# Attention scores on TensorE: two 64x128 matmuls per tile, or eight of 64x32

## The chip, the cores and the metric

The kernel runs on one core of a Trainium2 chip. The metric is the device time of one execution in microseconds (us); it is given as the median of several runs. A profile is of one execution. The engines are called as the profile calls them: PE (TensorE, matmuls), PEld (its weight loads), DVE (VectorE), ACT (ScalarE), POOL (GpSimd) and SP (SyncE, which only issues DMAs here). All data are fp32.

## What is computed

One layer with two residual blocks on x of shape (2, 2048, 256): a layer norm with a tanh recurrence, then a layer norm with an attention whose values and outputs are mixed from five small experts by top-2 gates. The change is in the attention, whose reference is, cut to what matters:

```python
q = (x @ Wq).reshape(b, t, h, dh).transpose(0, 2, 1, 3)      # 8 heads of 64
k = (x @ Wk).reshape(b, t, h, dh).transpose(0, 2, 1, 3)
...
v = jnp.einsum('bthe,btek->bhtk', wv, xv)
scores = jnp.einsum('bhid,bhjd->bhij', q * scale, k)
probs = jax.nn.softmax(scores, axis=-1)
attn = jnp.einsum('bhij,bhjd->bihd', probs, v)
...
out = jnp.einsum('bthe,bthk,ekd->btd', mask_o, attn, Wo)
```

## The kernel before

The recurrence comes first and takes about the first 130 us. The rest is the attention: 2 batches x 8 heads = 16 heads, each with 4 query blocks (QB = 512 queries), so 64 units. A unit runs over the 2048 keys in HC = 8 score tiles of 256 keys; there are 512 tiles.

A score tile `s` is [128, 2, 512] in PSUM: keys on partitions, two key blocks of 128 side by side (`o` = 0, 1), 512 queries. A head has only 64 features, so the 128 rows of the array are used as two halves. `keys` (L140) writes the keys of even blocks to partitions 0 to 63 of `k` and those of odd blocks to partitions 64 to 127. `queries` (L159) keeps `q` with one query block in the lower and another in the upper half, and `qs`, the same with the halves exchanged by two DMAs on SP's queue. So in `scores` (L634) the block `o` = 0 uses the lower 64 rows of the array and `o` = 1 the upper 64, with `q` or `qs` as the moving operand; each half has all 128 columns of the array for its 128 keys. The two halves write to different halves of the tile's second axis.

What then happens to a tile:

- `stage` (L645, ACT) copies it to SBUF as `p`, and `largest` (L655, DVE) keeps a running maximum over the unit's tiles, straight from PSUM.
- At a unit's end the maximum is turned (`pm`, L668, PE), reduced (L673, DVE) and spread again (`pt`, L683, PE; `top`, L686, ACT).
- Some turns later `subtract` (L693, POOL, some on DVE) and `exponential` (L696, ACT) make the probabilities in place.
- `products` (L706, PE) multiplies them by the values: per tile eight matmuls of 128 rows x 32 columns, four column quarters at a time, summed into `o` over the unit.
- `fold` (L718, a DMA on POOL's queue that adds in SBUF) adds two tiles of probabilities, and `sums` (L727, PE, 128 x 32 as well) takes the denominators `d` of the folded ones.
- A unit's result is turned (`po`, L759), weighed by the gates (L772) and added up in DRAM.

The order on all engines is written out by hand. The loop makes one turn for every two tiles: it issues the scores of two new tiles, then copies, maxima, subtractions, the listed extra work (`before`), `products` of two tiles from LAG = 6 turns earlier, `sums`, and more extra work (`behind`): `keys` (`pk`), `queries` (`pq`), `experts` (`pv`), transposes. Each engine takes its instructions in that order. There are 256 such turns. On PE a pair of score tiles stands therefore between matmuls of 128 x 32 (`o`, `d`, `pk`, `pq`, `pv`) or transposes of 128 x 128 (`pm`, `pt`, `po`). `s` has two buffers in PSUM (4 of the 8 banks); a new tile waits until ACT and DVE are done with the one two before it.

Of the kernel before, what the change touches and what calls it, by code (L numbers as in the profile page):

```python
# [14 lines left out]
P = 128  # L15
# [5 lines left out]
def rnn_then_switchhead_kernel(  # L21
# [15 lines left out]
    nc = tc.nc  # L37
    B, T, D = x.shape
    E, _, DH = Wv.shape
# [85 lines left out]
    k_of, q_of = {}, {}  # L125
# [502 lines left out]
    def scores(t):  # L628
        i, n = units[t // HC]
        c = t % HC  # L630
        ss = ps_s.tile([P, 2, QB], F32, tag="s", name=f"s{t}")
        for o in range(2):
            half = slice(o * DH, (o + 1) * DH)
            nc.tensor.matmul(  # L634
                ss[:, o, :],
                lhsT=k_of[i][half, c, :],
                rhs=q_of[i, n][o][half, :],
                start=True,
                stop=True,
            )  # L640
        return ss

    def stage(t, ss):
# [359 lines left out]
    with tc.manual_schedule():  # L1003
        for T in range(NT + LAG + 1):
# [8 lines left out]
            if old:  # L1013
                exponential(old[1])

            ss = [scores(t) for t in new]
            if new:
                stage(new[0], ss[0])
# [88 lines left out]
```

## Time and profile before

| | us |
|---|---|
| median of 5 runs (lowest, highest) | 1617.29 (1614.42, 1619.65) |
| the profiled execution | 1613.42 |
| its span, first to last instruction | 1611.7 |
| PE busy, matmuls | 1535.6 |
| L634, scores, busy (each half of the rows) | 512 |
| L706, products, busy | 491.5 |
| L727, sums, busy | 153.0 |
| L693, subtractions on POOL, busy | 1054.7 |

The profiled execution is 3.9 us below the median. Busy times of one engine's groups can overlap: two halves of the rows, or quarters of the columns, that run at once are each counted in their own group. A matmul's row in the trace gives its start well; its end is modelled. A shape such as 64*128 64x512 means 64 rows and 128 columns of the array, with 512 columns of 64 partitions moving. A releaser behind an arrow is what ended an engine's idle time.

### The profile page before, as it was taken

Reading aid. Unit: us, or ns where it says so; the run is one execution under the profiler, and the core shown is the slowest. Engines: PE = TensorE matmul, PEld = TensorE weight load, DVE = VectorE, ACT = ScalarE, POOL = GpSimd, SP = SyncE. Lnnn points to the kernel's source line nnn. Section 1 sums busy time; section 2 is a strip of 40 time slices with the busy share of each in tenths; the row PEclk is TensorE's granted clock in tenths of the full one; section 3 lists DMA queues with packets and bytes.
Section 4 is the critical chain, followed back from the end, with each engine's and each line's share of the span. In section 5 each row is a group of like instructions: output and inputs, shape, how many; then the busy total and the mean of one; then the engine's idle time right before and its main releaser. Section 6 shows DMA issues by size and latency. Waiting matters only on the chain.

```text
span 1611.7 us, 29233 instructions
## 1 busy us (share of the span) xinstructions
PE 1535.6 (95%) x11442; PEld 590.0 (37%) x11442; DVE 1297.6 (81%) x1808; ACT 1251.1 (78%) x1617; POOL 1283.4 (80%) x856
## 2 busy tenths in 40 slices
PE   6989899999999999999999999999999999999996
PEld 5974233333233333333334333333333333333233
DVE  7473889998988888888977769898989888888762
ACT  4664688888788888888887778888888888888861
POOL 3044698898888888999997868898989898889970
PEclk9999999999999999999999999999999999999999
DMA  5021468788888878778886767788888888888852
GB/s 162 1 106 32 117 156 196 162 187 163 183 170 167 179 161 176 162 172 164 176 184 157 168 142 187 156 177 174 177 166 174 177 169 172 165 170 165 171 131 86
DMA packets 86623, 252.26 MB, mean 157 GB/s; under 512 B 11920, under 2 KB 31184, under 8 KB 86480
## 3 DMA queue, kind: packets, MB, share of 16 engines
q0 software_dynamic: 43200, 163.60, 54.0%
q1 hardware_dynamic: 41648, 86.13, 17.2%
q8 instruction: 91, 1.49, 0.4%
q10 hardware_dynamic: 1632, 0.61, 0.1%
q14 instruction: 52, 0.43, 0.1%
HBM read 59.46 MB, written 50.33 MB: 68 GB/s over the span
## 4 chain that ended last, share of the span: by engine, by line
PE 66%; DVE 12%; DMA 7%; ACT 3%; issue 2%; POOL 2%; SPq 0%; DVEq 0%; ACTq 0%; POOLq 0%
PE s L634 23%; PE o L706 20%; PE d L727 6%; DMA p<-p 5%; DVE m L655 5%; PE pk L140 4%; PE pq L159 3%; ACT p L645 2%; PE pz L846 2%; DVE pro L772 2%; PE pt L683 2%; POOL p L693 1%; PE pm L668 1%; PE po L759 1%; PE pv L574 1%
## 5 line engine op out<-in xcount | busy, mean ns | idle before, releaser
L693 POOL TENSOR_TENSOR p<-p,top 128x1024 f32<-128x1024 f32 x381 | 1054.7, 3010 | 11.8 <-ACT top L686 11.7
L645 ACT COPY p<-s 128x1024 f32<-128x1024 f32 x512 | 510.9, 1011 | 152.5 <-DVE m L655 64.6
L696 ACT ACTIVATE p<-p 128x1024 f32<-128x1024 f32 x512 | 538.2, 1062 | 49.4 <-DVE p L693 37.3
L634 PE MATMUL s<-qs,k 64*128 64x512 f32 x1024 | 511.8, 617 | 6.4 <-ACT p L645 6.3
L634 PE MATMUL s<-q,k 64*128 64x512 f32 x1024 | 511.9, 617 | 3.9 <-ACT p L645 3.2
L706 PE MATMUL o<-p,v 128*32 128x512 f32 x4096 | 491.5, 597 | 10.2 <-DVE os L743 7.8
L655 DVE TENSOR_TENSOR m<-s,m 128x1024 f32<-128x1024 f32 x320 | 390.9, 1221 | 95.5 <-PE s L634 86.9
L718 POOL DMA_DIRECT2D p<-p x252 | 338.1, 1342 | 61.7 <-PE o L706 21.6
L706 PEld LDWEIGHTS o<-p,v 128*32 128x32 f32 x4096 | 113.6, 109 | 297.8 <-issue 155.3
L634 PEld LDWEIGHTS s<-qs,k 64*128 64x128 f32 x1024 | 169.0, 185 | 144.4 <-ACT p L645 46.2
L634 PEld LDWEIGHTS s<-q,k 64*128 64x128 f32 x1024 | 169.1, 185 | 138.6 <-issue 52.1
L693 DVE TENSOR_TENSOR p<-p,pt 128x1024 f32<-128x1024 f32 x131 | 158.5, 1210 | 0.1
L727 PE MATMUL d<-p,ones 128*32 128x512 f32 x1040 | 153.0, 593 | 5.0 <-DMA p<-p 4.9
L655 DVE TENSOR_TENSOR m<-s,p 128x1024 f32<-128x1024 f32 x64 | 78.4, 1224 | 55.3 <-ACT p L645 54.9
L814 POOL DMA_DIRECT2D yd<-pro x48 | 45.0, 937 | 91.7 <-DVE pro L772 89.4
L772 DVE TENSOR_TENSOR pro<-po,mr 128x1280 f32<-128x1280 f32 (+1 forms) x67 | 95.9, 1431 | 2.7
L619 DVE TENSOR_TENSOR xq<-xq,wp 128x1280 f32<-128x1280 f32 x60 | 89.3, 1488 | 2.3 <-DVE wp L617 0.2
L625 DVE TENSOR_REDUCE v<-xq 128x256 f32<-128x1280 f32 x60 | 88.6, 1477 | 0.0
L727 PEld LDWEIGHTS d<-p,ones 128*32 128x32 f32 x1040 | 37.2, 110 | 97.3 <-issue 77.5
L159 PE MATMUL pq<-xn2T,wq 128*32 128x512 f32 x512 | 63.2, 612 | 6.7 <-DVE rootd L434 6.7
L140 PE MATMUL pk<-xn2T,wk 128*32 128x512 f32 x512 | 61.5, 598 | 0.0
L673 DVE TENSOR_REDUCE mq<-pm 128x4 f32<-128x512 f32 x64 | 44.3, 692 | 18.3 <-PE pm L668 16.9
(172 smaller groups left out, 1468.5 us busy)
## 6 DMA issues: line engine op xcount, KB each, us to landing
p<-p POOLq DMA_DIRECT2D x252, 512.0 KB, 6.0
xq<-xvd SPq DMA_DIRECT2D x60, 640.0 KB, 5.4
yd<-pro POOLq DMA_DIRECT2D x48, 640.0 KB, 7.1
qs<-q SPq DMA_DIRECT2D x64, 128.0 KB, 2.7
yd<-pro SPq DMA_DIRECT2D x8, 640.0 KB, 4.1
y<-yd SPq DMA_DIRECT2D x8, 640.0 KB, 6.7
x<-in_x SPq DMA_DIRECT2D x16, 256.0 KB, 5.6
x1d<-x SPq DMA_DIRECT2D x16, 256.0 KB, 2.0
```

The source lines that it names most:

```text
L140: nc.tensor.matmul(pk[at_col : at_col + 32], lhsT=wk[:, kc, h * DH + g : h * DH + g + 32], rhs=xc[:, kc, c0 // 2 : (c0 + HC) // 2, o, :], ...
L159: nc.tensor.matmul(pq[at_col : at_col + 32, :], lhsT=wq[:, kc, h * DH + g : h * DH + g + 32], rhs=xn2T[:, kc, b, n * QB : (n + 1) * QB], s ...
L619: nc.vector.tensor_tensor(xq, xq, wp.unsqueeze(2).to_broadcast([P, 4, DH, E]), ALU.mult)
L634: nc.tensor.matmul(ss[:, o, :], lhsT=k_of[i][half, c, :], rhs=q_of[i, n][o][half, :], start=True, stop=True,)
L645: nc.scalar.copy(p, ss)
L655: nc.vector.tensor_tensor(m, ss, ring[t - 1] if c == 1 else m, ALU.max)
L693: eng.tensor_tensor(p, p, top.unsqueeze(1).to_broadcast([P, 2, QB]), ALU.subtract)
L696: nc.scalar.activation(ring[t], ring[t], AF.Exp)
L706: nc.tensor.matmul(o_of[u][at_col : at_col + 32, :], lhsT=v_of[i][:, 2 * c + o, g : g + 32], rhs=ring[t][:, o, :], start=c == 0, stop=c == ...
L718: nc.gpsimd.dma_start(out=ring[t], in_=ring.pop(t + 1), accum_op=ALU.add)
L727: nc.tensor.matmul(den_of[u][32 * g : 32 * (g + 1), :], lhsT=ones32, rhs=ring[(t, t1)[g // 2]][:, g % 2, :], start=first, stop=last, tile_ ...
L772: nc.vector.tensor_tensor(dst, po[:, s : s + n, 0:DH].unsqueeze(2).to_broadcast([P, n, E, DH]), mr[:, s : s + n].unsqueeze(3).to_broadcast ...
```

## The change

The matmul of each half is cut into four of 32 keys. Each writes 32 partitions of the score tile and is given its place in the array: row 0 or 64, and column 0, 32, 64 or 96. The same numbers are computed.

```diff
         for o in range(2):
             half = slice(o * DH, (o + 1) * DH)
-            nc.tensor.matmul(
-                ss[:, o, :],
-                lhsT=k_of[i][half, c, :],
-                rhs=q_of[i, n][o][half, :],
-                start=True,
-                stop=True,
-            )
+            for g in range(0, P, 32):
+                nc.tensor.matmul(
+                    ss[g : g + 32, o, :],
+                    lhsT=k_of[i][half, c, g : g + 32],
+                    rhs=q_of[i, n][o][half, :],
+                    start=True,
+                    stop=True,
+                    tile_position=(o * DH, g),
+                )
         return ss
```

## The prediction

> **What bounds the kernel now.** I read the page first, for who is busy and what the chain of waits is made of.
>
> ```profile
> span 1611.7 us, 29233 instructions
> ...
> PE 1535.6 (95%) x11442; PEld 590.0 (37%) x11442; DVE 1297.6 (81%) x1808; ACT 1251.1 (78%) x1617; POOL 1283.4 (80%) x856
> ...
> PE 66%; DVE 12%; DMA 7%; ACT 3%; issue 2%; POOL 2%; SPq 0%; DVEq 0%; ACTq 0%; POOLq 0%
> PE s L634 23%; PE o L706 20%; PE d L727 6%; DMA p<-p 5%; DVE m L655 5%; PE pk L140 4%; PE pq L159 3%; ACT p L645 2%; PE pz L846 2%; DVE pro L772 2%; PE pt L683 2%; POOL p L693 1%; PE pm L668 1%; PE po L759 1%; PE pv L574 1%
> ```
>
> The reader is to see that PE holds two thirds of the chain and that the changed line, L634, is its largest piece. Since a busy PE is not PE at its peak, I then asked for the busy times of the attention stretch alone (its columns: length, then busy time and count of PE, PEld, DVE, ACT and POOL, granted clock, DMA share, GB/s).
>
> ```profile
> 133.00:1545.00 1412.00, 1373.81 (x10059) 470.70 (x10063) 1191.68 (x1422) 1152.12 (x1374) 1219.22 (x782) 1.00 0.78 165
> ```
>
> PE stands still for 1412.0 - 1373.8 = 38.2 us of it (2.7%); the next engine, POOL, is free for 193 us. The granted clock is 1.00 throughout, so nothing is throttled. A nanosecond taken from PE's own sequence here is worth about 0.97 ns. Next the timeline of PE, for what its sequence costs beyond the streaming of columns; each row is start, length, engine, line, names, rows*columns of the array.
>
> ```profile
> 815.35 0.69 PE L634 MATMUL s<-q,k 64*128 64x512 f32 x1
> 815.35 0.69 PE L634 MATMUL s<-qs,k 64*128 64x512 f32 x1
> 815.88 0.59 PE L634 MATMUL s<-q,k 64*128 64x512 f32 x1
> 815.89 0.59 PE L634 MATMUL s<-qs,k 64*128 64x512 f32 x1
> 816.31 0.59 PE L634 MATMUL s<-q,k 64*128 64x512 f32 x1
> ...
> 816.74 0.59 PE L634 MATMUL s<-q,k 64*128 64x512 f32 x1
> ...
> 817.26 1.92 PE L140 MATMUL pk<-xn2T,wk 128*32 128x512 f32 x16
> ```
>
> Every matmul of the code is two passes in the trace (2048 records of s for 1024 instructions), each with its own weight load. The two row halves, q and qs, run side by side 7 ns apart, so a score tile costs two rounds, and a pair of tiles four. By the records' starts to the nanosecond, rounds follow each other after 429 ns (815.88 to 816.31), except the first (534) and the step out to pk (526). In the weight loads the same stretch reads:
>
> ```profile
> 815.35 0.18 PEld L634 LDWEIGHTS s<-q,k 64*128 64x128 f32 x1 [0.84 <-ACT p L696]
> ...
> 817.26 0.16 PEld L140 LDWEIGHTS pk<-xn2T,wk 128*32 128x32 f32 x8 [0.76 <-issue]
> 817.72 0.13 PEld L140 LDWEIGHTS pk<-xn2T,wk 128*32 128x32 f32 x4 [0.30 <-issue]
> ...
> 820.83 0.18 PEld L634 LDWEIGHTS s<-q,k 64*128 64x128 f32 x1 [0.84 <-ACT k L148]
> ```
>
> A load normally runs under the round before it. At 815.35, 817.26 and 820.83, where the array's division changes, it does not: the load starts with its own matmul, once the array has emptied.
>
> **The change part by part.** It removes 2 matmuls of 64 rows x 128 columns per score tile and adds 8 of 64 x 32, at 512 tiles. Nothing else moves: on DVE, ACT, POOL and SP order and waits are the same, no DMA or wait is added, and where a unit's qs half has a wait of its own it stands on the fifth piece instead of the second.
>
> *Streaming: 0.* If all eight pieces run side by side, a tile is still two rounds of 429 ns. The nearest row is pk (128*32): four 32-column pieces side by side, in rounds of 429 ns as well. Eight at once no row shows; that is the main risk and is priced below.
>
> *Entry: -81 ns.* Loading 128 columns makes the first round 534 ns; with 32 columns the first round of pk is 453 (817.264 to 817.717). 534 - 453 = 81. The median load, 186 against 110 ns, says the same (76). If the two row halves loaded one after the other, the exposed 453 - 429 = 24 ns would double, leaving 57; the rows speak against it, since q and qs load at once now. I take 81.
>
> *Exit: +40 ns.* Before the division changes, the last of the concurrent pieces must drain. Pieces start 6.6 ns apart. Out of one piece at a time (po to s) the step costs 96 ns beyond streaming, out of two (s to pk) 98, out of four (o to pt, o to s) 116. Six further pieces at 6.6 ns make 98 + 40 = 138. Lower bound 0 (the drain waits on the array alone), upper 6 x 9 = 54, from the slope 98 to 116 over two pieces.
>
> *The switch itself: 0.* The scores will then be 64*32, their neighbours 128*32 or 128*128, so the division still changes, now in rows only next to o, d, pk and pq. A change in rows alone is in the trace:
>
> ```profile
> 828.57 0.59 PE L634 MATMUL s<-qs,k 64*128 64x512 f32 x1
> ...
> 829.10 0.66 PE L668 MATMUL pm<-ident,mm 128*128 128x128 f32 x4
> ```
>
> It takes the same 526 ns, so I keep the switch.
>
> *Issue: 0.* 3072 more matmuls are 12,288 more records on PE. A pair of tiles then has 64 records (loads and matmuls) in about 1.9 us, 29 ns each; around 617 us PE takes 84 in 2 us, 24 ns each. Instruction transfers hold 0.5% of the DMA engines' time and may double; that is covered by their slack.
>
> *Reach: 0 to +188 ns per pair.* To load for the pair's second tile under the last round of its first, PE must look 57 records ahead: each matmul of the code being load, matmul, load, matmul, from the running second pass of piece one (record 4 of the tile's 32) to the first load of the next tile's eighth piece (record 61). With four pieces the trace shows it looking 25 ahead (from record 4 of pk's last sixteen to the fourth piece's first load of o, record 29). If it saw no further than now, those loads would begin only at a matmul's end, 592 instead of 429 ns after its start, plus 25 exposed: 163 + 25 = 188 ns, 256 times, 48 us. I take 0, since no row shows a limit; the end is kept for the range. [...]
>
> *Sum.* (-81 + 40) x 256 pairs = -10.5 us, x 0.973 = -10.2. Against the profiled execution's 1613.4 us this gives 1603.2. The median of the five runs is 3.9 us above that execution, so 1607.
>
> **The rivals.**
>
> 1. *PE's reach is too short* (slower): -10.5 + 48.1 = +37.6 us, so 1655; as the price goes from 0 to that, it decides from 41 ns per pair on. For it: twice as many pieces in flight as any row shows. Against it: the four-piece loads run under the round before without exception, and each column quarter still gets only four records per tile from each half.
>
> 2. *Row halves take turns when columns are split*: 512 x 0.858 = +439 us, about 2046. For it: no row combines both divisions. Against: the halves run concurrently at 128 columns, the quarters at 128 rows, without interference (429 ns in both).
>
> 3. *Switches vanish* next to 128*32 groups: some 190 of the exits (98 ns) and 160 of the entries (116) in the records have such a neighbour; 37 us, with the 20.7 of the entries and without most of the exit cost: about 1564. Against: the rows-only switch above.
>
> 4. *Another engine takes the gain*: a pair finishes 41 ns sooner but waits for ACT's copies or for POOL's folds; 1617. For it: the 38 us in which PE already waits. Against: every other engine has at least 190 us free in the stretch.
>
> **How the numbers follow.** My forecast has 0.60; its own range is 1597 (exit costs nothing, -20.7 x 0.973) to 1617 (entry 57, exit 54). Rival 1 has 0.16, rival 2 0.10, rival 3 0.06, rival 4 0.08. What a measurement here tells from no change is 0.2%, 3.2 us: faster means below 1614.1. The forecast has about 0.06 above that and rival 4 0.07, so same 0.13; faster 0.54 + 0.06 + 0.01 of rival 4 = 0.61; slower is rivals 1 and 2, 0.26. The range takes the forecast, rival 4 and rival 1 with its bound: 1595 to 1657; outside lie rivals 2 and 3, and a little of the others.
>
> **What would show it.** In the profile after: eight starts of s within 50 ns, 429 ns to the next eight; a first round of about 453 ns; loads of s of 106 to 110 ns; the step out of s about 566 ns (427 + 138); busy time of s near that of now. Rival 1 shows as the pair's third round starting late, rival 2 as four starts per round, rival 3 as loads of o under the last round of s. I am wrong if eight pieces share something that two halves or four quarters do not.

## The result and the profile after

| | median us | runs (lowest, highest) | ratio to before, 95% interval |
|---|---|---|---|
| before | 1615.41 | 64 (1610.99, 1619.85) | |
| changed | 1613.72 | 38 (1609.79, 1621.51) | 0.9991 (0.9985, 0.9998) |

The change made the kernel faster by 0.09%, some 1.5 us, where 10 us were forecast. That is inside what was called no change. The page of the changed kernel, same rows as before:

```profile
span 1609.2 us, 41521 instructions
...
PE 1529.8 (95%) x17586; PEld 540.7 (34%) x17586; DVE 1297.0 (81%) x1808; ACT 1250.8 (78%) x1617; POOL 1285.9 (80%) x856
...
PE 64%; DVE 14%; DMA 6%; ACT 4%; issue 3%; POOL 2%; SPq 0%; DVEq 0%; ACTq 0%; POOLq 0%
PE s L635 22%; PE o L708 19%; PE d L729 6%; DVE m L657 6%; DMA p<-p 4%; PE pk L140 4%; PE pq L159 3%; ACT p L647 3%; DVE pro L774 2%; PE pz L848 2%; PE pt L685 1%; POOL p L695 1%; PE pm L670 1%; PE po L761 1%; PE pv L574 1%
```

PE's share of the chain went from 66 to 64%, and DVE's from 12 to 14%: part of the chain has moved. The attention stretch (length; busy time and count of PE, PEld, DVE, ACT, POOL; clock, DMA share, GB/s):

```profile
133.00:1545.00 1412.00, 1368.62 (x16232) 420.62 (x16235) 1192.56 (x1424) 1154.12 (x1377) 1224.94 (x783) 1.00 0.78 166
```

PE is busy 5.2 us less in it (1373.81 before), and idle 5.2 us more: 43.4 against 38.2. (The stretch is the same in both, the work done in it only nearly.) PE's own work on a pair of score tiles is, in the timeline of PE, and below it the weight loads of the first and second round:

```profile
815.39 0.61 PE L708 MATMUL o<-p,v 128*32 128x512 f32 x4
815.93 0.63 PE L635 MATMUL s<-q,k 64*32 64x512 f32 x4
815.96 0.63 PE L635 MATMUL s<-qs,k 64*32 64x512 f32 x4
816.39 0.61 PE L635 MATMUL s<-q,k 64*32 64x512 f32 x4
...
816.82 0.61 PE L635 MATMUL s<-q,k 64*32 64x512 f32 x4
...
817.25 0.61 PE L635 MATMUL s<-q,k 64*32 64x512 f32 x4
817.27 0.61 PE L635 MATMUL s<-qs,k 64*32 64x512 f32 x4
817.81 1.92 PE L159 MATMUL pq<-xn2T,wq 128*32 128x512 f32 x16
```

```profile
815.93 0.12 PEld L635 LDWEIGHTS s<-q,k 64*32 64x32 f32 x4 [0.84 <-ACT k L148]
...
816.39 0.13 PEld L635 LDWEIGHTS s<-q,k 64*32 64x32 f32 x4 [0.28 <-issue]
816.42 0.13 PEld L635 LDWEIGHTS s<-qs,k 64*32 64x32 f32 x4
```

Eight pieces run side by side (the four of qs begin some 27 ns after the four of q), in rounds 429 ns apart. The first round takes 453 ns (815.935 to 816.388 in the records), the step out 566 (817.246 to 817.812). The prediction had 453 and 566. It is the same in all 256 pairs of tiles: the first round takes 453 or 454 ns in every one (533 or 534 before), and the median step out is 566 (526 before). So PE's sequence is as forecast, and the time is not. What PE waits for says where it went; these are waits, all but one of the weight loads (total us, times, longest), first of before, then of the changed kernel:

```profile
PEld s L634 <- ACT p L645: 86.8, 93, 2.7
...
PEld s L634 <- DVE m L655: 24.3, 41, 0.9
...
PEld o L706 <- DVE os L743: 19.9, 16, 1.6
```

```profile
PEld s L635 <- ACT p L647: 96.9, 104, 2.7
...
ACT p L647 <- DVE m L657: 62.6, 55, 1.8
...
PEld s L635 <- DVE m L657: 33.1, 49, 1.0
...
PEld o L708 <- DVE os L745: 22.0, 16, 1.7
```

Scores wait longer for ACT's copies and DVE's maxima to free a score buffer, 10.1 and 8.8 us more. A load can wait while matmuls run, so these sums are not all lost: the load at 815.93 above had waited 0.84 us, and from 815.39 on the last matmuls of `o` ran. Another count goes by the starts of the matmuls, and takes only steps that are over 115 ns longer than the usual one between the same two groups. By it PE's waits in the attention rose by 10 to 12 us, from some 45, and those of scores for DVE's maxima from about 1 to 6.0. That is as much as PE's sequence became shorter, in one execution of each kernel.

### The profile page after: what moved, and what is told of

Same layout as the page of the kernel before. It is cut to its first block, busy times and chain, and to the rows that moved or that the text cites. A ratio compares the mean times of both kernels' runs of the same rounds, so it can differ in the third digit from the quotient of the medians.

```text
span 1609.2 us, 41521 instructions
## 1 busy us (share of the span) xinstructions
PE 1529.8 (95%) x17586; PEld 540.7 (34%) x17586; DVE 1297.0 (81%) x1808; ACT 1250.8 (78%) x1617; POOL 1285.9 (80%) x856
## 4 chain that ended last, share of the span: by engine, by line
PE 64%; DVE 14%; DMA 6%; ACT 4%; issue 3%; POOL 2%; SPq 0%; DVEq 0%; ACTq 0%; POOLq 0%
PE s L635 22%; PE o L708 19%; PE d L729 6%; DVE m L657 6%; DMA p<-p 4%; PE pk L140 4%; PE pq L159 3%; ACT p L647 3%; DVE pro L774 2%; PE pz L848 2%; PE pt L685 1%; POOL p L695 1%; PE pm L670 1%; PE po L761 1%; PE pv L574 1%
## 5 line engine op out<-in xcount | busy, mean ns | idle before, releaser
L695 POOL TENSOR_TENSOR p<-p,top 128x1024 f32<-128x1024 f32 x381 | 1059.1, 3021 | 11.3 <-ACT top L688 11.3
L647 ACT COPY p<-s 128x1024 f32<-128x1024 f32 x512 | 510.9, 1011 | 153.0 <-DVE m L657 62.6
L698 ACT ACTIVATE p<-p 128x1024 f32<-128x1024 f32 x512 | 538.3, 1062 | 50.8 <-DVE p L695 38.2
L635 PE MATMUL s<-qs,k 64*32 64x512 f32 x4096 | 496.6, 596 | 7.7 <-ACT p L647 7.0
L635 PE MATMUL s<-q,k 64*32 64x512 f32 x4096 | 496.6, 596 | 4.4 <-ACT p L647 3.2
L657 DVE TENSOR_TENSOR m<-s,m 128x1024 f32<-128x1024 f32 x320 | 390.9, 1222 | 93.5 <-PE s L635 85.4
L720 POOL DMA_DIRECT2D p<-p x252 | 341.8, 1357 | 56.7 <-PE o L708 20.5
L635 PEld LDWEIGHTS s<-qs,k 64*32 64x32 f32 x4096 | 101.9, 106 | 157.2 <-ACT p L647 53.7
L635 PEld LDWEIGHTS s<-q,k 64*32 64x32 f32 x4096 | 101.9, 106 | 149.8 <-issue 59.7
```

Of the source, the lines that this page charges most:

```text
L635: nc.tensor.matmul(ss[g : g + 32, o, :], lhsT=k_of[i][half, c, g : g + 32], rhs=q_of[i, n][o][half, :], start=True, stop=True, tile_positi ...
L647: nc.scalar.copy(p, ss)
L657: nc.vector.tensor_tensor(m, ss, ring[t - 1] if c == 1 else m, ALU.max)
L695: eng.tensor_tensor(p, p, top.unsqueeze(1).to_broadcast([P, 2, QB]), ALU.subtract)
L698: nc.scalar.activation(ring[t], ring[t], AF.Exp)
L720: nc.gpsimd.dma_start(out=ring[t], in_=ring.pop(t + 1), accum_op=ALU.add)
```

## The experiments

Two theories were put against each other. A: PE's saved time becomes waits for other engines, whatever saves it. B: the change saves its 10 us, but its eight streams cost other engines or transfers as much. "Before" was timed again beside every group of runs (medians 1615.9 to 1616.5).

### PE shortened somewhere else

The loop of `products`, with W_O = 500 (or 464); in all tiles but a unit's first the products of the other columns are left out:

```diff
-                    o_of[u][at_col : at_col + 32, :],
+                    o_of[u][at_col : at_col + 32, 0 : W_O if c else QB],
...
-                    rhs=ring[t][:, o, :],
+                    rhs=ring[t][:, o, 0 : W_O if c else QB],
```

In the kernel before, with 500 columns:

> The kernel before with PE's sequence shortened in another place and nothing else touched: products of all tiles but a unit's first stream 500 instead of 512 columns (the last 12 queries of a block get the first tile's product only). 14 rounds per unit x 12 columns at 0.833 ns = 140 ns per unit, -9.0 us over 64 units, -35 ns per turn, about what the change takes from PE's sequence. Theory A (PE's saved time becomes waits for other engines, whatever saves it): ratio to before 0.998 to 1.000, about -1.5 us as the change gave. Theory B (the change saves its 10 us, but costs the other engines or the DMAs some 8 us by its eight streams): ratio near 0.995, -7 to -9 us.

In the changed kernel:

> The changed kernel with the same 500-column products (the last 12 queries of a block get the first tile's product only): -9.0 us of PE's sequence against the changed kernel, about -19 us against before. Theory A: again only a small part arrives, ratio to before 0.996 to 0.999. Theory B: the further 9 us arrive in full, ratio near 0.9935 (0.9991 - 0.0056).

In the kernel before, with 464 columns:

> The kernel before with products of 464 columns but for a unit's first tile (the last 48 queries of a block get the first tile's product only): 14 x 40 ns = 560 ns per unit, -35.8 us of PE's sequence. Theory A: the share that arrives falls or stays low as PE gets shorter; less than half, ratio 0.989 to 0.998. Theory B: ratio near 0.979, at least 30 us arrive.

| kernel | PE's sequence, us | median us | ratio to before | arrived |
|---|---|---|---|---|
| before, 500 columns | -9.0 | 1613.01 | 0.9977 (0.9967, 0.9988) | 3.7 us, 41% |
| changed, 500 columns | -19 | 1612.10 | 0.9970 (0.9958, 0.9983) | 4.8 us, 25% |
| before, 464 columns | -35.8 | 1605.14 | 0.9926 (0.9911, 0.9941) | 12.0 us, 33% |

(PE's sequence: the author's estimate, at 0.833 ns a column; in the trace of before, rounds of 512 columns follow each other after 429 ns, of 320 (`pv`) after 269, of 256 (`pz`) after 216. The -19 has the change's 10 us with it. Arrived: 1 minus the ratio, times before's 1616.5.) A nanosecond of PE in quite another place, with no new stream, load or shape, is worth 0.33 to 0.41 ns, not 0.97. The interval of the first row is wide (0.22 to 0.59), that of the last narrow (0.27 to 0.40). The first row lies a little above what theory A had said and far from B, the other two where A had said. Theory A holds for most of the loss. For all of it the change should have given some 4 us; it gave 1.5, so the first row leaves room for a small B.

### Four pieces of 64 columns

```diff
-            for g in range(0, P, 32):
+            for g in range(0, P, 64):
                 nc.tensor.matmul(
-                    ss[g : g + 32, o, :],
-                    lhsT=k_of[i][half, c, g : g + 32],
+                    ss[g : g + 64, o, :],
+                    lhsT=k_of[i][half, c, g : g + 64],
```

> Scores in four pieces of 64 rows x 64 columns, between the two kernels. By the terms of the prediction: entry, 64 columns loaded instead of 128 take 53 ns off (first round 480 instead of 534), exit with four pieces in flight about 98 + 13 = 111 to 116; net -36 to -40 ns per turn, as much as eight pieces. Both theories of the whole: theory A -1 to -2 us (0.999); theory B less cost than with eight streams, so ratio below that of the change, 0.995 to 0.998.

It took 1611.88 us, a ratio of 0.9969 (0.9957, 0.9980). PE's timeline of this kernel:

```profile
819.26 0.65 PE L635 MATMUL s<-q,k 64*64 64x512 f32 x2
819.27 0.65 PE L635 MATMUL s<-qs,k 64*64 64x512 f32 x2
819.74 0.60 PE L635 MATMUL s<-q,k 64*64 64x512 f32 x2
...
820.17 0.59 PE L635 MATMUL s<-q,k 64*64 64x512 f32 x2
...
820.60 0.59 PE L635 MATMUL s<-q,k 64*64 64x512 f32 x2
...
821.14 1.49 PE L159 MATMUL pq<-xn2T,wq 128*32 128x512 f32 x12
```

The first round is 480 ns and the step out 540: 53 off and 14 on, as worked out, 39 ns per turn against 41. Yet 5 us arrived, half of the 10. That is what theory B had said, not A. It was run again beside the changed kernel:

> The changed kernel once more, beside the four-piece one on the same chip. Theory A alone (both shorten PE by the same 39 to 41 ns per turn, both lose most of it): the two within 1.5 us. With a small cost of eight streams beside it: this one 2 to 4 us slower than four pieces.

> Four pieces of 64 columns once more: first 0.9969 of before against 0.9991 for eight pieces. If that difference is real: 2 to 4 us below the changed kernel of the same call, ratio to before 0.996 to 0.998.

The changed kernel took 1613.11, ratio 0.9986 (0.9971, 1.0001), the four pieces 1611.96, 0.9965 (0.9950, 0.9979). Four pieces are clearly faster than before both times. That they are faster than eight is likely (1.2 us here, which is A's range; 1.8 of the medians above and 2.3 under the reliefs below, which is about B's), but where the two were timed side by side the intervals overlap. A small B is therefore not excluded, and its cause stays open. It is not seen as slower work of another engine: the mean of DVE's maxima is 1222 ns with eight pieces and 1221 before, ACT's copies take 1011 and its exponentials 1062 in both, and POOL's subtractions take 3021 against 3010 but 3037 with four pieces.

### Other engines relieved, PE untouched

Three operations take 384 of their 512 columns, and the last quarter is left out (each edit also alone further down); PE's instructions stay the same:

```diff
-            nc.vector.tensor_tensor(m, ss, ring[t - 1] if c == 1 else m, ALU.max)
+            if c == 1:
+                nc.vector.tensor_tensor(m, ss, ring[t - 1], ALU.max)
+            else:
+                nc.vector.tensor_tensor(m[:, :, 0:384], ss[:, :, 0:384], m[:, :, 0:384], ALU.max)
...
-        eng.tensor_tensor(p, p, top.unsqueeze(1).to_broadcast([P, 2, QB]), ALU.subtract)
+        if eng is nc.gpsimd:
+            p, top = p[:, :, 0:384], top[:, 0:384]
+        eng.tensor_tensor(p, p, top.unsqueeze(1).to_broadcast([P, 2, 384 if eng is nc.gpsimd else QB]), ALU.subtract)
...
-        nc.scalar.activation(ring[t], ring[t], AF.Exp)
+        nc.scalar.activation(ring[t][:, :, 0:384], ring[t][:, :, 0:384], AF.Exp)
```

The kernel before:

> The kernel before with three engines relieved and PE untouched: running maxima (all but a unit's first and split one), subtractions on POOL and exponentials take 384 of the 512 columns, the rest is left as it is. That is about 0.26 us x 320 less on DVE, 0.25 us x 512 less on ACT, a quarter of 1055 us less on POOL. Theory A: PE waits some 45 us for them in the attention; the ratio to before is 0.97 to 0.99. Theory B says nothing of this run alone; it is the base of the next.

The changed kernel:

> The changed kernel with the same three reliefs (maxima, POOL's subtractions, exponentials on 384 of 512 columns). Theory A (other engines took the gain): against the relieved kernel before the change now brings most of its 10 us, 7 to 10 us, a ratio of 0.9935 to 0.9955 between the two. Theory B (the change itself costs PE or its neighbours): still 1 to 3 us, 0.998 to 0.9995.

Four pieces:

> Four pieces of 64 columns with the same three reliefs. PE's sequence is shorter by nearly the same as with eight pieces (entry 53 off, exit 14 on, 39 ns per turn against 41). Theory A: within 2 us of the relieved kernel with eight pieces. Theory B: 2 to 4 us faster than it.

| all three relieved | median us (lowest, highest) | ratio to before |
|---|---|---|
| before | 1576.61 (1575.29, 1578.16) | 0.9750 (0.9727, 0.9773) |
| changed | 1568.52 (1567.71, 1570.15) | 0.9701 (0.9678, 0.9724) |
| four pieces | 1566.21 (1564.92, 1569.76) | 0.9692 (0.9668, 0.9716) |

Now the same edit brings 8.1 us, 80% of what PE's sequence saves, and no run of one kernel reaches into the range of the other. The change was worth most of its forecast; the kernel around it could not use it. Which engine stood in the way, one at a time:

> The changed kernel with the maxima alone relieved (384 of 512 columns in all but a unit's first and split one), since the largest new wait of PE in the changed kernel's trace is for DVE's maxima at the score buffers: 6.0 us in 24 waits against 1.0 us before. If DVE is the taker: 5 us or more below the changed kernel, ratio to before 0.996 or lower. If it only stands where others would: ratio to before 0.997 to 0.999.

> The kernel before with the maxima alone relieved (384 of 512 columns in all but a unit's first and split one). The changed kernel with this relief took 1584.8 us. If DVE alone takes the change's gain: this one is 7 to 10 us slower than that, 1592 to 1595. If ACT or POOL take it as well: 1586 to 1590. If the gain is lost in PE's neighbourhood whatever the other engines do: within 2 us.

> The changed kernel with the exponentials alone on 384 of 512 columns, 0.25 us x 512 less on ACT. If DVE is the taker and ACT only stands behind it: less than 10 us below the changed kernel, ratio to before 0.993 or higher. If ACT's turn is as short of room as DVE's: 0.985 or lower.

> The changed kernel with POOL's subtractions alone on 384 of 512 columns, a quarter of POOL's largest work. POOL is the busiest engine after PE on the page. If it takes the gain: ratio to before 0.992 or lower. If DVE is the taker: 0.997 to 1.000.

> The kernel before with POOL's subtractions alone on 384 of 512 columns. The changed kernel with this relief took 1591.9 us. If DVE's maxima alone take the change's gain, POOL's relief does not bring it back: 1592 to 1594, within 2 us of that. If the gain is lost wherever DVE and POOL together keep PE waiting, and either relief brings it back: 1598 to 1601, 6 to 9 us above.

| relieved | before (lowest, highest) | changed (lowest, highest) | the change brings |
|---|---|---|---|
| nothing | 1615.41 | 1613.72 | 1.7 us of medians |
| DVE's maxima | 1592.70 (1591.22, 1594.48) | 1584.79 (1581.52, 1587.94) | 7.9 us |
| POOL's subtractions | 1596.56 (1595.96, 1599.08) | 1591.87 (1590.62, 1594.05) | 4.7 us |
| ACT's exponentials | not run | 1611.70 (1606.25, 1615.28) | |

Ratios to before: maxima 0.9851 (0.9835, 0.9868) and 0.9800 (0.9773, 0.9826); POOL 0.9883 (0.9863, 0.9903) and 0.9854 (0.9837, 0.9871), which overlap; ACT 0.9973 (0.9960, 0.9986). The two kernels of a row were not timed side by side. A quarter off most of the maxima, on an engine that is free for 219 us of the stretch, is worth 23.5 us to the kernel before (1616.20 beside it) and brings nearly the whole gain back. POOL's relief is worth 20 us and brings about half of it back; 1596.56 lies between the two forecasts of that run, and the intervals overlap, so this half is less sure. ACT's relief is worth 2 us in the changed kernel. Without the run of before it isn't shown whether it brings any of the change's gain back, but it removes 110 us of ACT's work for these 2 us. So DVE's maxima are the first taker, and POOL is probably a second one. The larger wait above names ACT, but ACT's copies wait for DVE's maxima themselves (62.6 us), and with the maxima relieved the scores of the changed kernel wait less for ACT's copies (82.9 us against 96.9). The utilization alone does not show this. The same 1356 us of the attention, in the kernel before and with its maxima relieved:

```profile
134.00:1490.00 1356.00, 1321.94 (x9714) 453.77 (x9710) 1147.39 (x1373) 1107.11 (x1322) 1170.01 (x752) 1.00 0.78 166
```

```profile
134.00:1490.00 1356.00, 1331.97 (x9824) 461.69 (x9828) 1082.15 (x1389) 1124.27 (x1340) 1187.57 (x763) 1.00 0.80 169
```

PE goes from 97.5 to 98.2% busy, hardly a difference to the eye, and its nanosecond from a sixth to four fifths of its worth. More work fits in: 9824 matmuls against 9714.

### DVE's order

The second maximum ahead of the first subtraction:

```diff
-            if fresh:
-                subtract(sub[0])
             if T % U_T and new:
                 largest(new[0], ss[0])
             if fresh:
+                subtract(sub[0])
                 subtract(sub[1])
```

> Four pieces of 64 columns, and in the one turn of four in which DVE subtracts, the second maximum of the turn is taken before the first subtraction instead of behind it, so that the score buffer is read 1.2 us earlier; the same work. If the wait of scores for DVE's maxima is what holds PE: 2 to 6 us below the four pieces alone (0.9969), ratio 0.993 to 0.9955. If DVE's total work holds it, or the later subtraction is missed elsewhere: 0.996 to 1.000 or worse.

1629.71 us, ratio 1.0083 (1.0069, 1.0098): 18 us slower than four pieces alone. The waits, first of the four pieces, then of this kernel:

```profile
PEld s L635 <- ACT p L647: 95.6, 102, 2.7
PEld o L708 <- ACT p L698: 95.3, 151, 1.8
...
ACT p L698 <- DVE p L695: 37.4, 53, 1.1
...
PEld s L635 <- DVE m L657: 28.7, 45, 1.0
...
PEld o L708 <- DVE os L745: 18.5, 15, 1.6
```

```profile
PEld s L635 <- ACT p L647: 109.2, 109, 2.7
PEld o L708 <- ACT p L698: 105.7, 186, 1.6
...
ACT p L698 <- DVE p L695: 91.3, 67, 1.7
...
PEld o L708 <- DVE os L745: 40.4, 37, 2.6
```

The wait of scores for the maxima fell from 28.7 to 5.4 us, as meant. In its place exponentials wait 54 us longer for DVE's subtractions, which now come a maximum (1.2 us) later, and `products` 10 us longer for exponentials. `products` also wait 22 us longer for `os` (L745), DVE's sum of the last unit's two halves, and scores 14 us longer for ACT's copies. The score buffer is thus not the only thing that DVE is late with. Less work on DVE helped, this other order of it did not.

## Why the prediction was wrong

The step that failed is the conversion: "A nanosecond taken from PE's own sequence here is worth about 0.97 ns". It was read off PE's idle share (2.7%) and off POOL's 193 us of free time. The runs put it at 0.33 to 0.41 for work taken from `products`, and at 0.15 for the change.

Point by point:

- *Streaming, 0.* Right: rounds of 429 ns with eight pieces.
- *Entry, -81 ns.* Right: 453 instead of 533 or 534.
- *Exit, +40.* Right: 566 instead of 526, and 540 with four pieces. From the start of the last piece the step out takes 519 or 520 ns in 238 of the 256 pairs of either kernel; that the pieces drain in this time is the author's reading of it.
- *The switch, 0.* Right: the first loads of scores still begin with their matmuls (both at 815.93), 543 ns after the last round of `o` (815.39), where rounds are 429 apart; out of `o` this step is 543 in the median, before and after. That the array is empty by then no row shows, since the ends are modelled.
- *Issue, 0.* Nothing late was seen: with 41,521 instructions the third round still comes 429 or 430 ns after the second in 230 of the 256 pairs (234 before).
- *Reach, 0.* Right, and rival 1 with it excluded: the next tile's eight loads run at 816.39 to 816.44, under the second round. If the records stand in the program as the prediction counts them, each piece's two passes one behind the other, PE looks at least 57 records ahead, and it starts all eight first passes (815.93 to 815.98) before any second (816.39). No trace here gives the order of the records in the program, so the 57 are an estimate.
- *Sum, -10.5 us of PE's sequence.* Right: by the measured steps it is 256 x (80 - 40) ns = 10.2 us, and in the relieved kernels 7.9 and 8.1 us of it arrive.
- *Rivals 2 and 3* did not occur. *Rival 4* did, and it was given 0.08, with "every other engine has at least 190 us free in the stretch" against it. That sentence was the error. The rival named ACT's copies and POOL's folds as takers; the runs point to DVE's maxima first, and to POOL's subtractions. Free time over a stretch did not say here who is late at a given moment: DVE is free for 219 us of it in the changed kernel (1412.0 - 1192.6), yet in a turn the scores wait for the buffer that DVE's maximum frees, and `products` for a subtraction and an exponential. With PE's earlier arrival these waits were longer: of scores for maxima 33.1 us against 24.3, of `products` for exponentials 99.5 against 90.3. The chain of before had shown 12% on DVE and 7% on DMA, 5% of it the folds, which the forecast read as small beside PE's 66%.

The measured 1613.72 lies between 1595 and 1657, but not because the forecast's mechanism carried it there: it lies near rival 4's 1617, and 1.9 us of the difference to that is the median of before, which was 1617.29 in five runs and is 1615.41 in 64.

That DVE takes most of the time is shown by the relieved pairs; for POOL it is likely. Which turns of a unit lose it is not: the reliefs were over all of them. The remaining difference between the change (1.5 us) and 500-column products (3.7 us), or four pieces (5 us), for about the same PE time is not explained; it is 2 to 3.5 us, with an uncertainty of about 2 us by the intervals.

## What to carry to other kernels

An engine that is busy 97% of a stretch, as PE was here (1373.8 of 1412.0 us), can still pass on only a third of what it saves (0.33 to 0.41 of the nanoseconds taken from `products`), or less (0.15 of the change's), when the other engines hand it its buffers with little to spare. Before a saving on one engine is forecast, it pays to ask what each wait of that engine would become if it arrived earlier, turn by turn; a cheap test is to shorten its work by a known amount elsewhere and see what arrives. Of the pieces tried, 64 columns had a longer first round than 32 (480 ns against 453) and a shorter step out (540 against 566), and did at least as well.

## What was not expected

A quarter off most running maxima on DVE, 81% busy, is worth 23.5 us, 1.5%. It takes 85.6 us of work from L655 (390.9 to 305.3 us), so a microsecond of it is worth 0.27 us. That is nearly as much as a microsecond of `products` on PE, 95% busy (12.0 us for 35.8, 0.33), and more than one of POOL's subtractions (20 us for 243, 0.08).

In the profile of the changed kernel with 500-column products the granted clock fell to 0.5 twice inside the attention, for 3.4 us each (at 834.4 and 1503.4 us), and rounds of scores took 853 to 855 ns instead of 429. In the kernel with DVE's order changed it did so once, at 178 us; in the other profiles only before the attention and in the last 50 us. No run was made to find out why.
